# Cross-attention with feed-forward on one core: loads on one queue, setup copies on ScalarE, and a last sum begun by TensorE

## The chip, the cores and the metric

The kernel runs on 1 core of one Trainium2 chip. The metric is the device time of one execution in microseconds; of the kernel before, three runs are given. A profile of one execution of it was taken as well. Its times are counted in microseconds (us) from the start of the span.

The engines are named as in the profile: PE is TensorE (matmuls; its weight loads, PEld, are listed apart), DVE is VectorE, ACT is ScalarE, POOL is GpSimd and SP is SyncE, which issues the loads and the stores.

## The reference

The input is x of 2 x 1024 x 256, a context of 2 x 77 x 256, a mask of 1024 x 77, and the weights of one attention layer with 16 heads and of eight feed-forward experts, of which only the first has a weight in the result. Cut to what matters:

```python
def attention(x, y, mask, Wq, bq, Wk, bk, Wv, bv, Wo, bo):
    q = (x @ Wq + bq).reshape(B, T, 16, 16)
    k = (y @ Wk + bk).reshape(B, 77, 16, 16)
    v = (y @ Wv + bv).reshape(B, 77, 16, 16)
    att = 0.25 * einsum('bthd,bThd->bhtT', q, k)
    att = softmax(att * mask - 1e10 * (1 - mask))
    return einsum('bhtT,bThd->bthd', att, v).reshape(B, T, 256) @ Wo + bo

def ffn(t, w1, b1, w2, b2, gamma, beta):   # expert 0 alone
    z = t + relu(t @ w1 + b1) @ w2 + b2
    return layernorm(z) * gamma + beta

x = x + attention(layernorm(x), ctx, mask, ...)
x = x + ffn(layernorm(x), ...)
```

All of it is float32.

## The kernel before

The 2048 rows of x are cut into eight tiles of 256 rows, called halves (h = 0 to 7); a half holds two rows on each of 128 partitions (n = 0, 1). Each half goes through one chain of stages. A stage is a short function that issues one group of instructions on one engine.

The attention side of a half: `xst`, `xrs`, `xnm`, `xn` (statistics, power and norm of x), `px` (turned by TensorE, L375), `xh` and `xl` (its high part rounded by ScalarE, L380, and the rest by VectorE, L385: a product in full precision is made of three matmuls, high by high, high by low, low by high), `pq` (query projection, L397), `qh` (query bias, L405), and for each n `sc` (scores, L417), `mu` (times the mask, DVE, L429), `bi` (plus the mask's bias, POOL, L438), then the maxima of eight heads each (`mx`, L443, and `ma`, L448), the subtraction for the first eight heads on DVE (`sb`, L453) and for the other eight on ScalarE (`sa`, L459, one instruction for each head), four turns (`tr`, L468) with four exponentials (`ex`, L473). Then `po` (times the values, L481; a column of ones beside the values gives the sums), `on` (division, L493 to L498), `pot`, `oh`, `ol`, `px1` (output projection, L529).

The feed-forward side: `yst` (residual sum and statistics), `yrs`, `ynm`, `tg` (norm), `py`, `yh`, `yl`, four up projections (`up`, L571) with `re` (relu, L580), `hh` (high part, L585) and `hl` (low part, POOL, L589), four down projections (`dn`, L600), then `zst` (sum with the residual, L612, and statistics, L329 to L333), `zrs` (power, POOL, L337), `znm`, `zt`, `zs` (norm, gamma and beta) and `out` (store, L642). The last half is stored in two parts, n = 0 and n = 1; for it the norm is made by two VectorE instructions for each part, L634 and L636.

What is done once: `wq`, `wk` are loaded through ScalarE's queue (L238, L239), everything else through SP's. The context is turned (`pc`, L278) and copied (`ct`, L284, DVE); the keys are projected (`pk`, L290) and spread into blocks with their bias by four VectorE instructions (`kb`, L296); the values are projected (`pv`, L308) and their bias, which was loaded to all 77 partitions, is added (`vs`, L311, DVE). The weights of the projections and of the feed-forward are cut into a high part (`fh`, L266, ScalarE) and a low part (`fl`, L269, POOL) once they have landed.

The order of the work on every engine is worked out beforehand by a planner (class `Stages`). Each stage has an engine, a cost, the stages it comes after, the buffers that it takes (rings, PSUM banks), and a rank; whenever an engine is free in the plan, the ready stage with the lowest rank is taken. The rank of a stage of half h is START[h], plus the costs on the path to it, plus TILE_LAG for the later stages, plus an offset for its name from the table LATER. The instructions are then issued in that order, and each engine takes its own in order; waits come from the data.

Fillers (`wm`, L210) are matmuls on zeros. They have the last rank of all, are ready one after the other by GAP, and take TensorE where the plan has nothing else for it.

## Time and profile before

| | us |
|---|---|
| median of 3 runs | 210.77 (210.18 to 211.86) |
| profiled execution, whole | 211.81 |
| its span, first to last instruction | 210.0 |

Some of the groups, as count and mean duration of one:

| group | count | mean, ns |
|---|---|---|
| POOL, bias of the scores, L438 | 32 | 1399 |
| POOL, low part of the hidden tile, L589 | 32 | 1289 |
| POOL, low parts of w1 and w2, L269 | 8 | 1294 and 1293 |
| ACT, subtraction for one head, L459 | 128 | 357 |
| ACT, high parts of w1 and w2, L266 | 8 | 624 and 626 |
| DVE, key blocks, L296 | 4 | 371 |
| DVE, values plus bias, L311 | 2 | 405 |
| DVE, last norm, L634 and L636 | 2 each | 489 and 484 |

Busy times are shares of the whole span. Since matmuls overlap, the busy time of PE tells where it had work and not how well it used it. In a row of the timeline the numbers are start and length in us, then engine, line, operation, the tile written, the tiles read, and in brackets how long the engine was idle before and what ended that.

### The profile page before, as it was taken

To read this page: it belongs to the slowest core of one execution; us is meant where nothing else is said; L and a number is where in the kernel's file an instruction comes from. 1 tells how busy PE (TensorE), PEld (TensorE's weight loads), DVE (VectorE), ACT (ScalarE), POOL (GpSimd) and SP (SyncE) were. 2 spreads that over 40 slices of the span, in tenths; PEclk is the share of its full clock that TensorE was granted. 3 is DMA by queue.
4 is the path that set the end of the run, shared out by engine and by line. 5 is a ranking of instruction groups with operands and counts; after the bars stand their busy time and mean duration, and the time that the engine had idled before them with its cause. 6 is when DMAs were issued, how large, how long until landed. Compare 5 with 4: busy or idle time off the path is not lost. (4 is left out here: it accounts for less than half of the span.)

```text
span 210.0 us, 4829 instructions
## 1 busy us (share of the span) xinstructions
PE 201.2 (96%) x1852; PEld 175.9 (84%) x1852; DVE 154.8 (74%) x336; ACT 155.3 (74%) x386; POOL 149.1 (71%) x151
## 2 busy tenths in 40 slices
PE   6999769999999999999999999999999999999995
PEld 1778556987996999799999778999988979999981
DVE  1678996999767992769999768999487667267234
ACT  3289998899894699993789997259997857624910
POOL 3469999899999967869998180197976573653741
PEclk9999997999999999999999999999999999999999
DMA  5997000000000000010000100001010000101011
GB/s 194 356 396 262 0 3 3 2 0 3 0 0 3 3 2 0 3 50 3 2 0 3 50 5 0 3 0 50 3 50 3 0 0 5 50 0 52 3 50 52
DMA packets 4807, 8.73 MB, mean 42 GB/s; under 512 B 662, under 2 KB 995, under 8 KB 4784
## 3 DMA queue, kind: packets, MB, share of 16 engines
q1 hardware_dynamic: 4496, 7.90, 10.3%
q10 hardware_dynamic: 288, 0.52, 0.7%
q8 instruction: 14, 0.23, 0.5%
q14 instruction: 9, 0.07, 0.1%
HBM read 6.33 MB, written 2.10 MB: 40 GB/s over the span
## 5 line engine op out<-in xcount | busy, mean ns | idle before, releaser
L438 POOL TENSOR_TENSOR u<-u,mb 128x616 f32<-128x616 f32 x32 | 44.1, 1399 | 9.5 <-DVE u L429 9.1
L589 POOL TENSOR_TENSOR hl<-h,hh 128x512 fp32r<-128x512 f32 x32 | 40.9, 1289 | 10.2 <-ACT hh L585 8.7
L571 PE MATMUL ps<-yh,w1h 128*128 128x256 f32 x128 | 37.4, 292 | 0.0
L473 ACT ACTIVATE pT<-ps 77x512 f32<-77x512 f32 x64 | 34.2, 593 | 3.9 <-PE ps L468 3.9
L600 PE MATMUL ps<-w2h,hh 128*128 128x256 f32 x128 | 37.0, 289 | 0.0
L468 PE MATMUL ps<-ident,u 128*77 128x128 f32 x256 | 34.9, 281 | 2.1 <-DVE u L453 1.3
L571 PE MATMUL ps<-yl,w1h 128*128 128x256 f32 x128 | 36.3, 283 | 0.0
L571 PE MATMUL ps<-yh,w1l 128*128 128x256 f32 x128 | 36.1, 282 | 0.0
L600 PE MATMUL ps<-w2h,hl 128*128 128x256 f32 x128 | 35.8, 279 | 0.0
L600 PE MATMUL ps<-w2l,hh 128*128 128x256 f32 x128 | 35.8, 279 | 0.0
L468 PEld LDWEIGHTS ps<-ident,u 128*77 128x77 f32 x256 | 29.5, 150 | 6.6 <-DVE u L453 2.2
L459 ACT ACTIVATE u<-u,mx 128x77 f32<-128x77 f32 x128 | 33.7, 357 | 0.6 <-DVE mx L448 0.6
L580 ACT ACTIVATE h<-ps,cols 128x256 f32<-128x256 f32 x64 | 26.6, 471 | 7.9 <-DVE ot L493 3.8
L571 PEld LDWEIGHTS ps<-yh,w1h 128*128 128x128 f32 x128 | 24.4, 191 | 1.7 <-issue 0.9
L429 DVE TENSOR_TENSOR u<-ps,mk 128x616 f32<-128x616 f32 x32 | 24.1, 792 | 2.0 <-PE ps L417 2.0
L600 PEld LDWEIGHTS ps<-w2h,hh 128*128 128x128 f32 x128 | 24.3, 190 | 1.2 <-issue 1.1
L571 PEld LDWEIGHTS ps<-yl,w1h 128*128 128x128 f32 x128 | 24.5, 191 | 0.2 <-DVE yl L554 0.2
L571 PEld LDWEIGHTS ps<-yh,w1l 128*128 128x128 f32 x128 | 24.5, 191 | 0.0
L600 PEld LDWEIGHTS ps<-w2l,hh 128*128 128x128 f32 x128 | 24.1, 188 | 0.0
L600 PEld LDWEIGHTS ps<-w2h,hl 128*128 128x128 f32 x128 | 24.1, 188 | 0.0
L585 ACT ACTIVATE hh<-h 128x512 fp32r<-128x512 f32 x32 | 20.0, 634 | 5.1 <-PE ps L600 4.5
L481 PE MATMUL ps<-pT,vb 77*32 77x256 f32 x256 | 16.8, 388 | 0.1
(96 smaller groups left out, 427.2 us busy)
## 6 DMA issues: line engine op xcount, KB each, us to landing
x<-in_x SPq DMA_DIRECT2D x8, 256.0 KB, 5.5
out<-tg SPq DMA_DIRECT2D x7, 256.0 KB, 2.0
wst<-in_L_ffn_w SPq DMA_DIRECT2D x4, 256.0 KB, 5.4
wst<-in_w SPq DMA_DIRECT2D x4, 256.0 KB, 6.0
rows<-in_rows SPq DMA_DIRECT2D x1, 512.0 KB
mk<-in_mask SPq DMA_DIRECT2D x1, 308.0 KB, 4.9
wq<-in_wq ACTq DMA_DIRECT2D x1, 256.0 KB
wk<-in_wk ACTq DMA_DIRECT2D x1, 256.0 KB, 4.6
```

The costliest lines, as they stand in the source:

```text
L429: nc.vector.tensor_tensor(us[h, n][:, 8 * s : 8 * s + 8].rearrange("p (b h) t -> p b h t", b=2), ps[:, b0 : b0 + 2, :W].rearrange("p b (h ...
L438: nc.gpsimd.tensor_tensor(v, v, mb[:, h % HPB, n].unsqueeze(1).to_broadcast([P, 8, T]), ALU.add)
L459: nc.scalar.activation(u, u, AF.Identity, bias=mx[:, k : k + 1])
L468: nc.tensor.transpose(pt[:T, j], us[h, n][:, k], ident)
L473: nc.scalar.activation(pTs[h][:, i, :, n], pss.pop(("t", h, n, i))[:T], AF.Exp)
L481: nc.tensor.matmul(pos[h, s][r, e], lhsT=vb[:, h // HPB, k], rhs=pTs[h][:, 2 * s + e, j].rearrange("k n t -> k (n t)"), start=True, stop=True,
L571: nc.tensor.matmul(pz[:, i], lhsT=w[:, c, j * P : (j + 1) * P], rhs=v[:, c], start=(k == 0), stop=(k == 5))
L580: nc.scalar.activation(t[:, i], pz[:, i], AF.Relu, bias=b1[:, 2 * q + i : 2 * q + i + 1])
L585: nc.scalar.activation(hh[h, q], hs[h, q], AF.Copy)
L589: nc.gpsimd.tensor_tensor(hl[h, q], hs.pop((h, q)), f(hh[h, q]), ALU.subtract)
L600: nc.tensor.matmul(pys[h, ns[0]][:, n], lhsT=v[h, q][:, i, n * P : (n + 1) * P], rhs=w[:, j], start=(q == 0 and n == ns[0] and i == 0 and ...
```

## The change

Loads. `wq` and `wk` are loaded from SP too, and the order there is x0, context, wk, mask, wq, x1, wv, x2, value bias, wo and then as before. The small table of columns (biases, b1, block mask) is packed behind the mask, in one load of 640 columns, and has no load of its own. The value bias is loaded to one partition.

Setup. The context copy and the key blocks are made by ScalarE (the key blocks with a scale and a bias from columns, the bias multiplied beforehand by one small VectorE instruction, `bkm`). The value bias is added by a third matmul, a row of ones by the bias row, and the values are then copied by ScalarE.

Last half. Each of its two parts gets a sum that TensorE begins with the residual (`dt`, an identity matmul of 256 columns), so the VectorE addition goes. The centring (`zc`) is a stage of its own that does not come after the power. The low parts of its last two hidden tiles are made by VectorE instead of POOL.

Order. The subtraction on ScalarE is two stages of four heads, one for each of the turns that read it; the maximum of the first eight heads comes after the first bias stage alone; all START, LATER, TILE_LAG and several costs have other values, and the planner's delay between two engines no longer falls away where two stages merely begin with the same letter. Fillers are 256 columns wide in place of 512, there are 100 in place of 40, ready every 0.3 in place of 0.44, with a cost of 0.11 in place of 0.3.

```diff
-START = [0.0, 19.8, 51.7, 142.9, 83.1, 131.4, 163.5, 235.6]
+START = [0.0, 73.7, 67.8, 216.8, 128.7, 156.8, 213.7, 271.1]
...
-WARM = 40
+WARM = 100
...
-GAP = 0.44
-TILE_LAG = 11.6
+GAP = 0.3
+TILE_LAG = 19.8
...
-        return 0.0 if k[0] == u[0] else HOP[self.all[k]["eng"] + self.all[u]["eng"]]
+        return 0.0 if self.name(k) == self.name(u) else HOP[self.all[k]["eng"] + self.all[u]["eng"]]
...
+    LAST = [(NH - 1, q) for q in (2, 3)]
...
+        nc.tensor.matmul(bank(("wm", i))[:, :256], lhsT=zero[:, :P], rhs=zero, start=True, stop=True)
...
+    mkc = const([P, a["mask"].shape[1]], "mkc")
+    mk = mkc[:, : HPB * 2 * T].rearrange("p (h n t) -> p h n t", h=HPB, n=2)
+    cols = mkc[:, HPB * 2 * T :]
...
-    load_matrix("wq", "wq", "hh", nc.scalar)
-    load_matrix("wk", "wk", "hl", nc.scalar)
...
-        nc.vector.tensor_copy(ct, pcv)
+        nc.scalar.activation(ct, pcv, AF.Copy)
...
+    def k_bias():
+        nc.vector.tensor_tensor(
+            bkm, bk.unsqueeze(2).to_broadcast([P, 2, 2]), bm.unsqueeze(1).to_broadcast([P, 2, 2]), ALU.mult
+        )
+
+    def k_blocks(c):
+
+        for e in range(2):
+            nc.scalar.activation(
+                kb[:, :, c, e], pss["k"][:, c], AF.Identity, bias=bkm[:, c, e : e + 1], scale=bm[:, e : e + 1]
+            )
...
+        nc.tensor.matmul(pv, lhsT=one, rhs=bv, start=False, stop=True)
+
+    def v_copy(b):
+        nc.scalar.activation(vb[:, b, :, :D], pss.pop(("v", b)).rearrange("p (h d) -> p h d", d=D), AF.Copy)
...
+    def s_sub_act(h, n, i):
+        for k in heads(i):
             u = us[h, n][:, k]
-            nc.scalar.activation(u, u, AF.Identity, bias=mx[:, k : k + 1])
+            nc.scalar.activation(u, u, AF.Identity, bias=mxs[h, n, 1][:, k : k + 1])
...
+        eng = nc.vector if (h, q) in LAST else nc.gpsimd
+        eng.tensor_tensor(hl[h, q], hs.pop((h, q)), f(hh[h, q]), ALU.subtract)
...
-        nc.vector.tensor_tensor(y2, y2, tg[h][:, n0:n1], ALU.add)
+        if h < NH - 1:
+            nc.vector.tensor_tensor(y2, y2, tg[h][:, n0:n1], ALU.add)
         stats(y2, f"z{h}_{n0}")
+
+    def z_center(h, n):
+        y2 = pys[h, n][:, n]
+        nc.vector.scalar_tensor_tensor(y2, y2, sts[f"z{h}_{n}"][0][:, 0, 0:1], gamma, ALU.subtract, ALU.mult)
+
+    def f_first(h, n):
+
+        pys[h, n] = bank(("dt", h, n), (P, 2, E))
+        nc.tensor.matmul(pys[h, n][:, n], lhsT=ident, rhs=tg[h][:, n], start=True, stop=False, skip_group_check=True)
...
-            half("mx", "V", 0.1 + 0.08 * (H - ACT_HEADS[h]), [("bi", n, 0), ("bi", n, 1)], s_max, n, lag=lag)
...
+            half("mx", "V", 0.74, [("bi", n, 0)], s_max, n, lag=lag)
...
+                if i >= 2:
+                    half("sa", "S", 1.0, [("ma", n)], s_sub_act, n, i, lag=lag)
```

Of the table LATER, the offsets that the text speaks of: `fl` (low parts of w1 and w2) from 64.8 to 127.9, `up` from 25.5 to 80.7.

## The prediction

> **What bounds the kernel now.** I read the page first, then the busy times by stretch, the timeline of the opening and of the end, and the waits of TensorE. The page says that TensorE is the engine to follow, and the stretches say where it is not full.
>
> ```profile
> PE 201.2 (96%) x1852; PEld 175.9 (84%) x1852; DVE 154.8 (74%) x336; ACT 155.3 (74%) x386; POOL 149.1 (71%) x151
> ```
> ```profile
> 0.00:12.20 12.20, 10.00 (x36) 5.83 (x37) 5.87 (x20) 4.71 (x9) 4.32 (x14) 1.00 0.82 291
> 12.20:30.00 17.80, 14.52 (x142) 11.51 (x141) 16.01 (x34) 17.02 (x45) 16.84 (x23) 1.00 0.42 157
> 30.00:110.00 80.00, 79.56 (x785) 71.26 (x784) 65.06 (x136) 66.86 (x173) 71.97 (x68) 0.98 0.01 5
> 110.00:203.40 93.40, 92.99 (x877) 85.72 (x877) 64.38 (x139) 66.70 (x163) 54.82 (x47) 1.00 0.05 18
> 203.40:210.00 6.60, 4.08 (x19) 1.56 (x16) 3.50 (x11) 0.00 (x0) 1.10 (x2) 1.00 0.12 41
> ```
>
> Columns: length, then PE, PEld, DVE, ACT, POOL busy. From 30 to 203.4 us TensorE is busy for 172.55 of 173.4 us: work added to it there lengthens the kernel, and work taken from others there gives nothing. What can be won lies in three places: before the first query projection (12.25 us), between 12.2 and 30, and after 203.4.
>
> The front, from the timeline (start, length, engine, line):
>
> ```profile
> 4.54 0.75 DVE L329 BATCH_NORM_STATS2 st_x<-x 128x6 f32<-128x256 f32 x2 [3.39 <-DMA x<-in_x]
> 5.91 2.34 PE L210 MATMUL ps<-zero 128*128 128x512 bf16 x5
> 6.34 0.47 DVE L284 COPY ct<-ps 128x308 f32<-128x308 f32 x1
> 7.22 1.09 ACT L357 ACTIVATE xn<-x,nm_x,rs_x 128x256 f32<-128x256 f32 x2 [1.85 <-DVE nm_x L342]
> 8.04 2.18 PE L290 MATMUL ps<-ct,wk 128*128 128x154 f32 x8
> 10.05 0.60 PE L375 MATMUL ps<-ident,xn 128*128 128x128 f32 x4
> 12.25 0.47 PE L397 MATMUL ps<-xh,wqh 128*128 128x256 f32 x1
> ```
>
> The first tile of x lands at 4.54. Its normed rows are ready at 8.31, but their turn on TensorE starts at 10.05, behind the key projection (8.04). That one had its input at 6.81 and stood behind five filler matmuls: TensorE takes its queue in order.
>
> The opening and the end:
>
> ```profile
> 21.95 1.03 PE L210 MATMUL ps<-zero 128*128 128x512 bf16 x4
> 24.25 1.10 PE L468 MATMUL ps<-ident,u 128*77 128x128 f32 x8 [1.27 <-DVE u L453]
> 28.91 0.80 PE L417 MATMUL ps<-kb,qs 32*128 32x154 f32 x12 [1.80 <-ACT pT L473]
> ```
> ```profile
> 202.75 0.43 DVE L612 TENSOR_TENSOR ps<-ps,tg 128x256 f32<-128x256 f32 x1 [3.87 <-PE ps L600]
> 203.14 0.28 PE L600 MATMUL ps<-w2h,hl 128*128 128x256 f32 x1
> 203.99 0.42 DVE L612 TENSOR_TENSOR ps<-ps,tg 128x256 f32<-128x256 f32 x1
> 205.44 0.55 POOL L337 TENSOR_TENSOR rs_z<-rs_z,mhalf 128x1 f32<-128x1 f32 x1 [0.74 <-DVE rs_z L333]
> 206.79 0.48 DVE L636 SCALAR_TENSOR_TENSOR tg<-ps,rs_z,x 128x256 f32<-128x256 f32 x1
> ```
>
> Idle or filled with nothing in the opening: 1.03 + 1.27 + 1.80 = 4.1 us. At the end, 3.85 us pass from the last matmul's end (203.42) to the last scale's end (207.27), then 2.7 us of store and closing.
>
> **The change, part by part**, against the profiled run (211.81 us, 210.0 of it span; the median of the three runs is 210.77, 1.04 below).
>
> *Loads.* x0 shared the wires with wq, issued by ScalarE at the same moment. Around 4 to 6 us the DMA table shows some 400 GB/s, so 256 KB less ahead of it is 0.64 us: x0 lands at 3.9. c (154 KB) follows 0.4 later, 4.3, where before it ended TensorE's wait at 5.37. wq now comes behind c, wk and mask with columns (about 730 KB, 1.8 us after 4.54): 6.4 us; its two copies (0.63 and 0.69) end near 8, and it is needed at 10. x1 moves behind mask and wq, 0.3 MB or 0.8 us later; its rows waited 1.2 us for ScalarE (0.30 and 1.66 of statistics end near 10.4, xn starts at 11.70), which hides it. The ACT issues (0.41 and 0.39) vanish, two issues of 0.38 to 0.43 go to SP ahead of all later loads, and the column load (0.35) goes. Total bytes stay, so the last weights land as before.
>
> *Front.* From 3.9, statistics and norm take the same 3.77: 7.7. The context turn (0.75) from 4.3, its copy and the key projection (2.18) end near 8.0. Then turn, high part, low part take the 2.20 of before (10.05 to 12.25): query projection at 10.2, 2.05 earlier. One filler in the way costs some 0.2; I take **-1.8**, bounds 0 (fillers as badly placed as the five above) and -2.05.
>
> *Copies on ScalarE.* The context copy (0.47 on DVE) falls into ScalarE's idle time (4.71 of 12.2 busy). The key blocks were four DVE instructions of 0.371 and become four on ScalarE of 154 elements with two column operands: between the 128x77 row with one (0.357) and the 128x256 row with two (0.603), 1.4 to 2.4 in all; near 8 to 10.5 ScalarE waited 2.38 us for the turn, so they cost nothing unless the high part (0.60) stands behind a pair of them, then up to 1.2. The value copies (two, about 0.45 by the 128x256 rows) fall into the opening, where ScalarE is busy for 17.02 of 17.80.
>
> The Trainium skill ("ScalarE: Activation LUTs", Rules for kernel authors) speaks against this part: it sends plain adds and multiplies to VectorE. By its figures (about 0.19 us fixed, 0.09 for each column operand, 0.83 ns an element) one key block is, as an estimate, 0.50 us, so 2.0 for four against 1.5 before; in this trace it is the load of the two engines in that stretch that decides.
>
> *Value bias by matmul.* Two more matmuls of 256 columns: two of this kind took 1.03 (L308), so 0.5 each. One lies in the front's idle time (behind it are fillers), the other in the dense opening: **+0.5**, bounds 0 and +1.0.
>
> *Opening.* The maximum of the first eight heads no longer stands behind the second bias add (1.40 on POOL), the ScalarE subtraction is cut into two fours, so a turn may follow the first four (1.05 earlier), and the weights' low parts (1.29 each on POOL; one, at 14.81, stands ahead of the first bias add at 17.73) sink in rank. Against it: ScalarE and POOL (16.84 of 17.80) are both nearly full. Bounds: -4.1 and, with the value copies on the path, +0.9. I take half of what is idle, **-2.0**.
>
> *Middle.* The order is redrawn; TensorE's instructions stay. 0 with the bounds -2 (TensorE hardly idles, only its mixing of kinds can tighten) and +6 (rival below).
>
> *Last half.* Two identity matmuls of 256 columns on a TensorE that is full: **+0.9** (0.43 to 0.52 each by the same L308 row), bounds 0 and +1.0. They replace the DVE add (0.43 and 0.42). The last low parts on DVE (0.69 for 1.29) fall into its 3.87 us of waiting; without that cover they would put 0.69 ahead of the statistics. After the last matmul remain: a hop of 0.25 (as from 12.00, the end of xl, to 12.25), statistics 0.43, and from there as 203.22 to 204.70 shows for the first part (aggregate, epsilon, power), then 0.1 and the scale of 0.48; the centring (0.49) fits beside the power (0.55). That is 2.35 for 3.85; DVE still holds the first part's centring, up to 0.5. **-1.2**, bounds -1.5 and -0.8.
>
> *Fillers.* 100 for 40, half as wide. Before, 18 were left for the end and finished at 208.23, short of the store. At 0.108 each, 60 left over would run 6.5 us after the last matmul, against some 5.3 for the rest: 0, up to +1.5.
>
> Sum: -1.8 + 0.5 - 2.0 + 0.9 - 1.2 = -3.6; 208.2 for the profiled run, **207.2** for the median.
>
> The clock: seven fillers take 3.17 us from 1.21 (0.43 apart), five take 1.24 from 10.49 (0.22 apart), while the granted clock reads 1.00 throughout. So TensorE speeds up between 7.6 and 10.5. The Trainium skill ("TensorE: Matmul & The Clock Gate", Part 1) has a rule that speaks against the change: half rate until about 3.4 us of sustained activity, and again after as long an idle time; thinner fillers, planned every 0.30 us where they ran 0.43 long every 0.44, are less sustained. If the fast rate came only after the first query projection, that one (12 matmuls 0.12 apart, 1.44) would take twice as long by these two spacings, and the sum would be -2.2.
>
> **The rivals.**
>
> A, the forecast, 207.2 (205.7 to 209.2): 0.46, of it 0.40 faster and 0.06 same.
>
> B, more: the opening gives all 4.1 and the middle 1.5: -7.2, **203.6**. For it: maxima, subtractions and turns may all start earlier. Against it: 172.55 of 173.4. 0.17, all faster.
>
> C, the opening stays, since ScalarE and POOL are its bound: -1.6, **209.2**. For it: 17.02 of 17.80. 0.12; 0.03 faster, 0.09 same.
>
> D, slower: POOL becomes the bound, because the low parts of the feed-forward weights come too late. There are eight at 1.29 (10.3 us). For it: POOL is the fullest helper from 30 to 110 (71.97 of 80), and the lateness of these copies goes from 64.8 to 127.9, while that of the up projection that reads them goes from 25.5 to 80.7. Against it: the four of w1 ended at 43.0 and the first up projection began at 52.0, the four of w2 ended at 52.9 and the first down projection began at 67.3, so 9 and 14 us can be lost first. Each copy that TensorE stands and waits for is +1.29: three (3.9) eat the whole gain, and from there D decides; five, w1's four and one of w2's, are +6.45, **213.7**; all eight 217.5. 0.20, all slower.
>
> E, the change does at the front what it says, but the fillers left over end the kernel: +1.5, **208.7**. For it: 60 more of them. 0.05, same.
>
> **How the numbers follow.** 207.2 is A's. Range 203.4 to 213.0: below it lies what is left of B if the middle gives its whole 2 (0.07), above it D from five whole copies on (0.13 of its 0.20; the other 0.07 is the fifth half hidden, +5.8, 213.0). Over 1% faster (under 208.66): 0.40 + 0.17 + 0.03 = 0.60; within 1%, about what a measurement of this kernel can tell from no change: 0.06 + 0.09 + 0.05 = 0.20; slower 0.20.
>
> **What would show it.** x0 landing near 3.9 and the first L397 row near 10.2; TensorE busy for over 16 of the 17.8 us that follow; TensorE as dense from 30 us to the last matmul as before; 2.4 to 2.9 us from the last matmul to the last scale; low-part copies done before the first up projection, with no wait of TensorE for POOL. Wrong: a first query projection after 11.5, waits of TensorE for POOL or ScalarE of several us between 30 and 200, or fillers that end after the last store.

## The result, and the profile after

| | before | after |
|---|---|---|
| median, us | 211.31 (20 runs, 210.18 to 212.95) | 212.45 (20 runs, 211.26 to 214.72) |
| profiled execution, whole | 211.81 | 212.64 |
| its span | 210.0 | 210.8 |

The ratio is 1.0059, with a 95% interval of 1.0038 to 1.0080: the change made the kernel slower by 0.6%. The forecast was 207.2, faster with a chance of 0.60. Medians are of all runs, ratios leave out the runs in which the chip was in a slower state, and e9 and e16, which were profiled in that state, are read by their times alone.

The page's line of busy times for the kernel after:

```profile
PE 202.5 (96%) x1920; PEld 180.3 (86%) x1920; DVE 151.7 (72%) x331; ACT 159.2 (76%) x393; POOL 146.5 (69%) x149
```

TensorE is as busy as before, 202.5 against 201.2, in 68 more matmuls. Sixty of them are fillers, so the sum hides what is useful. The stretches of the kernel after (length, then PE, PEld, DVE, ACT, POOL busy with their counts, granted clock, DMA):

```profile
0.00:12.12 12.12, 10.16 (x55) 6.59 (x56) 5.22 (x21) 7.36 (x15) 4.79 (x15) 1.00 0.84 293
12.12:30.00 17.88, 15.77 (x156) 13.99 (x156) 13.77 (x29) 15.16 (x37) 16.69 (x22) 1.00 0.44 152
...
30.00:60.00 30.00, 29.39 (x327) 23.59 (x325) 29.11 (x55) 29.16 (x82) 29.46 (x29) 1.00 0.01 2
...
110.00:200.10 90.10, 90.10 (x837) 84.57 (x835) 59.07 (x133) 62.80 (x150) 50.44 (x44) 1.00 0.04 16
200.10:202.60 2.50, 2.50 (x25) 2.24 (x24) 1.94 (x7) 1.07 (x2) 1.24 (x2) 1.00 0.00 0
...
206.07:210.80 4.73, 1.11 (x11) 0.75 (x8) 1.67 (x5) 0.00 (x0) 0.55 (x1) 0.89 0.08 29
```

Two rows matter. From 200.1 to 202.6 TensorE is "full", but with fillers, as the timeline of the end shows (start, length, engine, line):

```profile
199.98 0.28 PE L600 MATMUL ps<-w2h,hl 128*128 128x256 f32 x1
200.11 2.69 PE L212 MATMUL ps<-zero 128*128 128x256 bf16 x23
201.81 0.48 DVE L643 SCALAR_TENSOR_TENSOR tg<-ps,rs_z,x 128x256 f32<-128x256 f32 x1 [0.19 <-POOL rs_z L339]
202.63 0.60 PE L623 MATMUL ps<-tg,ident 128*128 128x256 f32 x2
...
205.79 0.28 PE L600 MATMUL ps<-w2h,hl 128*128 128x256 f32 x1
205.91 1.27 PE L212 MATMUL ps<-zero 128*128 128x256 bf16 x10
206.11 0.43 DVE L331 BATCH_NORM_STATS2 st_z<-ps 128x6 f32<-128x256 f32 x1 [2.29 <-PE ps L600]
207.69 0.48 DVE L643 SCALAR_TENSOR_TENSOR tg<-ps,rs_z,x 128x256 f32<-128x256 f32 x1 [0.33 <-POOL rs_z L339]
```

Between the last part's first sum (done at 200.1) and the identity matmul that begins its second sum (202.63) stand 23 fillers, in the queue of an engine that takes its work in order. And in the row from 30 to 60 all four engines are busy for over 29 of 30 us, where before DVE had 25.75 and ACT 27.68.

The front, from the timeline of the kernel after:

```profile
3.47 0.75 DVE L331 BATCH_NORM_STATS2 st_x<-x 128x6 f32<-128x256 f32 x2 [2.38 <-DMA x<-in_x]
3.99 0.75 PE L283 MATMUL ps<-ident,c_sb 77*128 77x77 f32 x4 [0.18 <-DMA c_sb<-in_c]
5.26 1.32 PE L295 MATMUL ps<-ct,wk 128*128 128x154 f32 x8
5.83 1.09 ACT L359 ACTIVATE xn<-x,nm_x,rs_x 128x256 f32<-128x256 f32 x2 [0.62 <-DVE nm_x L344]
7.18 0.60 PE L377 MATMUL ps<-ident,xn 128*128 128x128 f32 x4
...
7.54 0.63 ACT L271 ACTIVATE wqh<-wq 128x512 fp32r<-128x512 f32 x1 [0.61 <-DMA wq<-in_wq]
8.07 1.58 ACT L307 ACTIVATE kb<-ps,bkm,mkc 128x154 f32<-128x154 f32 x4
...
9.53 0.61 ACT L382 ACTIVATE xh<-ps 128x512 fp32r<-128x512 f32 x1
10.52 1.09 PE L314 MATMUL ps<-wv,ct 128*77 128x256 f32 x4
10.55 0.66 DVE L387 TENSOR_TENSOR xl<-ps,xh 128x512 fp32r<-128x512 f32 x1
...
12.12 0.38 PE L399 MATMUL ps<-xh,wqh 128*128 128x256 f32 x1
```

x lands at 3.47 (4.54 before) and is turned by 7.78 (10.65 before, by the rows of 10.05 and 0.60), yet the first query projection begins at 12.12 (12.25). The turned rows wait 1.75 us for ScalarE, which waits for wq until 7.54 and then makes the four key blocks; and TensorE has the value projections in front.

In what follows, **TensorE's lag** at a time t is t less the time that the computation's own matmuls done by then take at the pitch at which they follow each other densely; fillers count nothing. It is worked out from the matmul records, and less lag at the same t is more work done.

| t, us | lag before | lag after |
|---|---|---|
| 34 | 20.73 | 18.81 |
| 40 | 21.00 | 20.85 |
| 60 | 22.79 | 22.94 |
| 200 | 28.71 | 27.93 |

So TensorE was 1.9 us ahead at 34 us, lost that by 40, won 0.9 between 60 and 200, lost 2.5 in the fillers at 200, paid 0.86 for two identity matmuls, and won 1.74 behind the last matmul (206.07 to 208.18, where it was 3.85): +0.8, the spans' difference. Part of the 1.9 isn't the change's: in the execution before, the granted clock of TensorE was 0.81 from 28 to 32 us and 0.76 from 32 to 36, in the one after 1.00.

### The profile page after: what moved, and what is told of

It reads as the page before. It is cut to its first block, busy times and chain, and to the rows that moved or that the text cites. A ratio compares the mean times of both kernels' runs of the same rounds, so it can differ in the third digit from the quotient of the medians.

```text
span 210.8 us, 4973 instructions
## 1 busy us (share of the span) xinstructions
PE 202.5 (96%) x1920; PEld 180.3 (86%) x1920; DVE 151.7 (72%) x331; ACT 159.2 (76%) x393; POOL 146.5 (69%) x149
## 4 chain that ended last, share of the span: by engine, by line
PE 82%; DMA 8%; DVE 3%; ACT 3%; issue 1%; SPq 1%; POOL 0%; POOLq 0%
PE ps L600 22%; PE ps L570 22%; PE ps L467 12%; PE ps L480 8%; PE ps L528 6%; PE ps L419 5%; DMA x<-in_x 4%; PE ps L399 3%; DMA mkc<-in_mask 2%; DMA wst<-in_L_ffn_w 2%; PE ps L212 2%; PE ps L544 2%; ACT pT L472 1%; DVE u L431 1%; ACT u L458 1%
## 5 line engine op out<-in xcount | busy, mean ns | idle before, releaser
L589 POOL TENSOR_TENSOR hl<-h,hh 128x512 fp32r<-128x512 f32 x30 | 38.7, 1294 | 11.9 <-ACT hh L584 10.8
L472 ACT ACTIVATE pT<-ps 77x512 f32<-77x512 f32 x64 | 35.1, 591 | 10.5 <-PE ps L467 10.5
L600 PE MATMUL ps<-w2h,hh 128*128 128x256 f32 x128 | 37.7, 295 | 0.0
L458 ACT ACTIVATE u<-u,mx 128x77 f32<-128x77 f32 x128 | 34.7, 359 | 1.1 <-DVE mx L449 0.9
L579 ACT ACTIVATE h<-ps,mkc 128x256 f32<-128x256 f32 x64 | 26.6, 470 | 8.8 <-PE ps L570 7.7
L467 PEld LDWEIGHTS ps<-ident,u 128*77 128x77 f32 x256 | 29.0, 147 | 4.9 <-issue 2.5
L431 DVE TENSOR_TENSOR u<-ps,mkc 128x616 f32<-128x616 f32 x32 | 24.2, 791 | 7.8 <-PE ps L419 7.8
L339 POOL TENSOR_TENSOR rs_z<-rs_z,mhalf 128x2 f32<-128x2 f32 (+1 forms) x9 | 6.0, 666 | 27.9 <-DVE rs_z L335 27.5
L570 PEld LDWEIGHTS ps<-yh,w1h 128*128 128x128 f32 x128 | 24.5, 191 | 1.0 <-issue 1.0
L570 PEld LDWEIGHTS ps<-yl,w1h 128*128 128x128 f32 x128 | 24.5, 191 | 0.0
L570 PEld LDWEIGHTS ps<-yh,w1l 128*128 128x128 f32 x128 | 24.5, 191 | 0.0
```

The lines of the kernel that those rows point to most:

```text
L431: nc.vector.tensor_tensor(us[h, n][:, 8 * s : 8 * s + 8].rearrange("p (b h) t -> p b h t", b=2), ps[:, b0 : b0 + 2, :W].rearrange("p b (h ...
L458: nc.scalar.activation(u, u, AF.Identity, bias=mxs[h, n, 1][:, k : k + 1])
L467: nc.tensor.transpose(pt[:T, j], us[h, n][:, k], ident)
L472: nc.scalar.activation(pTs[h][:, i, :, n], pss.pop(("t", h, n, i))[:T], AF.Exp)
L570: nc.tensor.matmul(pz[:, i], lhsT=w[:, c, j * P : (j + 1) * P], rhs=v[:, c], start=(k == 0), stop=(k == 5))
L579: nc.scalar.activation(t[:, i], pz[:, i], AF.Relu, bias=b1[:, 2 * q + i : 2 * q + i + 1])
```

## The experiments

All ratios are to the kernel before, with 95% intervals. All but e7 are edits of the kernel after. `move(stages, behind)` puts stages behind another one in the finished order of issue; nothing else of the order changes. Times of stages are of the profiled executions.

### The fillers at the end: e1

```diff
-        for key in st.order():
+        order = st.order()
+        order = [key for key in order if key[0] != "wm" or key[1] < 67]
+        for key in order:
```

> The changed kernel in its own order, without the 33 fillers from the 67th on (23 of them stand on TensorE between the first part's down projections and the identity matmul of the second part, 200.1 to 202.6 us). Theory (the fillers are the cost): the plan left a hole there, because the second part's sum may only begin when one of two sums is given back, and filled it; on the chip the data of the second part are there, so TensorE goes straight on: the identity matmul near 200.2, the end 2.3 to 2.5 us earlier, about 1.1 to 1.2% less than the changed kernel. Rival (the hole is real): the second part waits for a low part, a bank or a scale until about 202.5; then TensorE stands idle instead, and the time moves by less than 0.3 us.

Measured: 210.62, ratio 0.9963 [0.9933, 0.9993]. The timeline of e1 at the same place:

```profile
199.75 0.28 PE L600 MATMUL ps<-w2h,hl 128*128 128x256 f32 x1
199.87 0.59 PE L623 MATMUL ps<-tg,ident 128*128 128x256 f32 x2
...
205.07 0.48 DVE L643 SCALAR_TENSOR_TENSOR tg<-ps,rs_z,x 128x256 f32<-128x256 f32 x1 [0.33 <-POOL rs_z L339]
```

The identity matmul follows at once: nothing on the chip had held it, neither data nor bank. What held it was the plan, which allows two sums open at a time:

```python
SUMS = 2
half("dt", "P", 0.45, ["yb"], f_first, *ns, lag=lag, banks=[[("zs",) + ns]], sums=("dn", SUMS))
```

Half 3's sum and the last half's first part held both places, so the second part's `dt` had to come, in the plan, after the scale of the first. TensorE was free in the plan meanwhile, and the planner issued fillers there. They are real instructions; on the chip 2.5 us of them ran where useful work was ready. This is shown: the last scale came 2.6 us earlier (205.55 for 208.18). The step stands in one place: TensorE's own matmuls have the same order in both kernels, the same matmul starts 0.24 us earlier in e1 from 24 us on to 198, and 2.76 earlier from the identity matmul on.

### The other fillers, the copies, the queue of wq and wk: e10, e11, e12, e14

```diff
# e10, in place of the 67 of e1
+        order = [key for key in order if key[0] != "wm" or key[1] < 27]
# e11, on e1; the copies of the values likewise
-        nc.scalar.activation(ct, pcv, AF.Copy)
+        nc.vector.tensor_copy(ct, pcv)
...
-            nc.scalar.activation(
-                kb[:, :, c, e], pss["k"][:, c], AF.Identity, bias=bkm[:, c, e : e + 1], scale=bm[:, e : e + 1]
+            nc.vector.tensor_scalar(
+                kb[:, :, c, e], pss["k"][:, c], bm[:, e : e + 1], bkm[:, c, e : e + 1], ALU.mult, ALU.add
# e12, on e1; these two are no longer loaded from SP
+    load_matrix("wq", "wq", "hh", nc.scalar)
+    load_matrix("wk", "wk", "hl", nc.scalar)
```

e14 is e10, e11 and e12 together.

> The kernel of e1 without the 40 fillers between the first query projection and 50 us as well (7 at 14 to 15.4, 16 at 25 to 28.7, 16 at 36.7 to 38.6, 1 at 49.5). If fillers in those places also delay work that is ready, as they do at the end: up to 1 us earlier than e1 (ratio 0.991 to 0.994). If TensorE really has to wait there: within 0.3 us of e1.

> The kernel of e1 with the context copy, the key blocks and the value copies on VectorE again (same order, same loads). In the changed kernel the key blocks (1.58 us on ScalarE, 8.07 to 9.65) stood ahead of the high part of x0 that was ready at 7.8. If that is what held the front: the first query projection is only as early as the value projections ahead of it let it (11 to 11.5 instead of 12.1), and the end comes 0.5 to 1 us earlier. If the place of the copies is without weight: within 0.4 us of e1.

> The kernel of e1 with the loads of wq and wk issued by ScalarE again, ahead of everything, as in the kernel before. x0 then shares the wires with wq and lands near 4.5 instead of 3.5, the context 1 us later; wq lands near 4.7 instead of 7.5, so the high and low parts of wq and of x0 no longer stand behind it. If the earlier x0 is worth something: the first query projection and the end come later by up to 1 us. If the wait for wq cancels it: within 0.4 us of e1.

> The changed kernel without the fillers behind the 27th, with the turned mask column's copy, the key blocks' and the values' copies on VectorE, and with the query and key weights' loads issued by ScalarE's queue. If the small gains seen of each alone add: 0.9963 without late fillers, 0.0009 for the other fillers, 0.0014 for the copies and 0.0033 for the second queue, a ratio of 0.9907 or about 209.4 us. If they are the same gain seen three times (each only makes the front start earlier or TensorE's queue shorter, and the opening takes it back): 0.993 to 0.995, 209.8 to 210.3 us.

Measured: e10 210.43, 0.9954 [0.9923, 0.9985]; e11 210.15, 0.9949 [0.9927, 0.9972]; e12 209.81, 0.9930 [0.9901, 0.9959]; e14 209.98, 0.9945 [0.9923, 0.9968]. All overlap with e1's interval and with each other. Neither the engine of the early copies nor the queue of wq and wk has an effect that these runs tell from none, and together they give no more than one of them. What all of them share is the removal of the late fillers, and all of them beat both kernels, by 0.4 to 0.7% under the kernel before. The fillers at 25 to 28.7 and at 36.7 to 38.6, which e10 leaves out as well, held nothing: the same matmul of TensorE starts 1.18 us earlier in e10 than in the kernel after at 24 us, ahead of them, and 1.25 earlier at 40, behind them.

### The front alone: e2 and e8

```diff
# e2
+        move([("kb", 0), ("kb", 1)], ("xh", 0))
+        move([("pv", 0), ("vs", 0), ("pv", 1), ("vs", 1)], ("pq", 0))
+        move([("xst", 2), ("xrs", 2)], ("xl", 0))
# e8, 14 more fillers ahead of the first query projection
+        for i in range(14):
+            order.insert(order.index(("pq", 0)), ("more", i))
```

> The changed kernel in its own order, except at the front: the key blocks come after the high part of the first tile on ScalarE, the value projections after the first query projection on TensorE, the third tile's statistics after the first low part on VectorE. Theory (order at the front ate the gain of the earlier load): the first query projection starts at 9.6 to 10.2 instead of 12.12, and if TensorE is the bound from there on, the end comes 1.9 to 2.5 us earlier. Rival (the opening is bound by the other engines): the first query projection starts as early, but the progress of TensorE at 40 us and the end move by less than 0.7 us.

> The changed kernel in its own order, with 14 more fillers of 0.108 us on TensorE ahead of the first query projection, so that it starts 1.5 us later. If TensorE's front sets the time, as the prediction's front term took it: 1.5 us slower, 0.7%. Rival (the opening has a chain of its own, and the front has slack): at 22 us TensorE is as far as without them, and the end moves by less than 0.4 us.

e2: 214.24, 1.0121 [1.0071, 1.0172]; e8: 213.89, 1.0120 [1.0080, 1.0160]. ScalarE's timeline in e2:

```profile
8.21 0.60 ACT L382 ACTIVATE xh<-ps 128x512 fp32r<-128x512 f32 x1 [0.50 <-PE ps L377]
8.71 1.59 ACT L307 ACTIVATE kb<-ps,bkm,mkc 128x154 f32<-128x154 f32 x4
...
13.69 0.38 ACT L318 ACTIVATE vb<-ps 77x256 f32<-77x256 f32 x1 [1.12 <-PE ps L315]
15.29 0.38 ACT L318 ACTIVATE vb<-ps 77x256 f32<-77x256 f32 x1 [1.22 <-PE ps L315]
15.57 1.08 ACT L359 ACTIVATE xn<-x,nm_x,rs_x 128x256 f32<-128x256 f32 x2
16.55 0.82 ACT L407 ACTIVATE qs<-ps,mkc 128x256 f32<-128x256 f32 x2
```

The first query matmul came at 8.87 as meant and the rest by 12.2, but its bias on ScalarE (L407) came at 16.55, behind two copies of values that TensorE now made late. The wait moved one stage on. The Trainium skill ("TensorE: Matmul & The Clock Gate", Part 1, Architectural detail) says that ScalarE and VectorE take their queues strictly in order; these rows agree: the bias had its input by 12.3 and ran 4.2 us later. e8 holds the front back by 1.3 to 1.5 us and is 0.6% (1.3 us) slower than the kernel after by the two ratios, whose intervals just touch. Its trace is level with the kernel after at 22 us (lag 14.47 for 14.38) and 0.44 behind at 34 (19.25 for 18.81); the table of the next section shows that these 0.44 go with a later load and not with the fillers. So whether the front held back costs time, or has slack, stays open.

### What is late in the opening, one stage at a time: e3, e4, e5, e6

```diff
# e3
+        move([("fh", k) for k in range(4, 8)], ("yl", 0))
# e4
+        move([("xb", 2), ("xb", 0), ("xb", 1)], ("bi", 2, 1, 1))
# e5
+        for h in (3, 4, 5, 6):
+            move([("xb", h)], order[order.index(("px1", h)) - 25])
# e6
+        move([("xst", 4)], ("mu", 0, 1, 1))
```

`xb` is the addition of the output projection's bias to x, on POOL.

> The changed kernel in its own order, except that the four high parts of w2 (0.62 us each on ScalarE, at 20.4 to 23.0) come after the first low part of the feed-forward input, near 48 us. If ScalarE bounds the opening: turns and exponentials come up to 2.5 us earlier and the end 1 to 2.5 us. If POOL bounds it, or the chain through mask, bias and maximum: less than 0.4 us, perhaps worse by as much, since ScalarE has them to do later.

> The changed kernel in its own order, except that three output-bias adds on POOL (1.28 us each; two of them at 16.1 to 18.7 stand ahead of the first score bias, which began at 18.64 while its input was there at 17.3; one at 21.3) come after the eighth bias pair, near 39 us. If POOL bounds the opening: the first score bias starts at 17.3, the first turn 1.3 to 2.6 us earlier, the end 1 to 2.5 us earlier. If ScalarE bounds it: less than 0.4 us.

> The changed kernel in its own order, except that the output-bias adds of halves 3 to 6 (1.28 us each on POOL, at 31.3, 39.2, 40.5 and 47.9 us) come shortly before the output projection that needs them, after 60 us. Theory (all helpers are full in the opening, POOL the most: it works without a pause from 16.1 to 60): with 5.1 us less on POOL before 60, TensorE gets its turns earlier and is 1 to 4 us further at 60 us, and the end comes 1 to 3 us earlier. Rival (the opening goes by ScalarE, or by all three alike): less than 0.5 us at 60 us, and the adds moved into the middle cost what they gain.

> The changed kernel in its own order, except that the statistics of half 4 on VectorE, which stood idle 1.93 us for the load of that half (landed at 19.9), come after the two mask products that stood behind them (21.5 to 23.0). Theory (a load in the way of the masks holds the opening, as the chain of waits says): masks start at 20.0, scores at 20.8 instead of 22.3, and the end comes 0.8 to 1.5 us earlier. Rival (POOL is full anyway): the masks come earlier, but the second pair of bias adds starts at 22.6 as before, and the end moves by less than 0.4 us.

Measured: e3 214.33, 1.0153 [1.0101, 1.0205]; e4 214.82, 1.0127 [1.0070, 1.0185]; e5 213.3, 1.0107 [1.0073, 1.0141]; e6 213.68, 1.0110 [1.0068, 1.0153]. None is faster than the kernel after. In e4, e5 and e6 the lag at 60 us was 24.93, 23.61 and 24.93 instead of 22.94. In e3 it was 17.47 instead of 18.81 at 34 us and 21.13 instead of 22.40 at 52.

e3's lead looks like the gain of four copies less on ScalarE, and it isn't. The rows of the kernel after (first fence) and of e3 (second) show what the first turn waited for:

```profile
19.90 0.75 DVE L331 BATCH_NORM_STATS2 st_x<-x 128x6 f32<-128x256 f32 x2 [1.93 <-DMA x<-in_x]
...
23.72 1.10 PE L467 MATMUL ps<-ident,u 128*77 128x128 f32 x8 [0.61 <-DVE u L453]
24.42 1.08 ACT L472 ACTIVATE pT<-ps 77x512 f32<-77x512 f32 x2 [1.38 <-PE ps L467]
```
```profile
18.58 0.75 DVE L331 BATCH_NORM_STATS2 st_x<-x 128x6 f32<-128x256 f32 x2 [1.16 <-DMA x<-in_x]
...
22.40 1.10 PE L467 MATMUL ps<-ident,u 128*77 128x128 f32 x8 [0.61 <-DVE u L453]
23.10 1.08 ACT L472 ACTIVATE pT<-ps 77x512 f32<-77x512 f32 x2 [2.48 <-PE ps L467]
```

The statistics of half 4 stand on VectorE ahead of the second pair of masks and of the first subtraction, and wait for their load. In e3's execution it landed 1.32 us earlier, the first turn came 1.32 earlier, and ScalarE, with four copies less, only waited longer for it (2.48 for 1.38). e10, which has the four copies in their old place, has the same lead. The table takes the kernels in which TensorE's own matmuls have the order of the kernel after, and gives how much later (+) or earlier (−) than there the same matmul starts:

| | statistics of half 4 | of that wait for the load | first turn | at 24 us | at 40 | at 60 | at 198 |
|---|---|---|---|---|---|---|---|
| after | 19.90 | 1.93 | 23.72 | 0 | 0 | 0 | 0 |
| e1 | 19.09 | none | 23.48 | −0.23 | −0.26 | −0.24 | −0.24 |
| e3 | 18.58 | 1.16 | 22.40 | −1.32 | −1.32 | −0.61 | −0.24 |
| e4 | 21.07 | 2.07 | 24.88 | +1.16 | +1.13 | +1.85 | +2.48 |
| e5 | 19.77 | none | 24.20 | +0.48 | +0.48 | +0.50 | +0.50 |
| e8 | 20.33 | 1.13 | 24.15 | +0.43 | +0.44 | +0.45 | +1.20 |
| e10 | 18.70 | 0.86 | 22.54 | −1.18 | −1.25 | −1.25 | −1.25 |

Where VectorE waits for the load, the distance at 24 us is the difference in its landing to within 0.02 us (after, e3, e4, e8, e10), though none of these edits moves a load. And what stands at 24 us is carried to the end in e1, e5 and e10; e4 and e8 lose more on the way, and e3 loses its lead. So e5 shows more than its lag says: 5.1 us less on POOL before 60 us moved TensorE by nothing between 24 and 198 us. e6 takes the wait out of the way of the masks, but the statistics then stand (22.62) ahead of the first subtraction, which comes at 23.50 instead of 22.88.

e3 keeps its lead until ScalarE makes the four copies, at 54.7 to 56.9, and loses 1.07 of 1.31 us between 58 and 65 us, where e10 loses nothing. Two stretches of e3:

```profile
28.00:52.00 24.00, 23.39 (x253) 19.28 (x251) 23.32 (x45) 23.57 (x66) 23.23 (x27) 1.00 0.01 2
52.00:62.00 10.00, 9.87 (x107) 6.44 (x104) 8.77 (x16) 10.00 (x27) 8.77 (x8) 1.00 0.01 2
```

Where the four copies run, ScalarE (the fourth busy time) has no idle time at all, and VectorE and POOL have 1.2 each: more work on ScalarE there holds TensorE up. That the median is 0.9% over the kernel after's is not explained by the trace, whose span (210.9) is level with it; the profiled execution was the fastest of e3's six (212.66).

### The first softmax ahead: e9, e13, e15, e16, e17

Each of these orders moves several stages of half 0's chain forward and others back, e9 on e1, the others on e14. Of each the moves that matter; e17 has all of e15:

```diff
# e9
+        move([("kb", 0), ("kb", 1)], ("xh", 0))
+        move([("xst", 1), ("xrs", 1), ("xst", 2), ("xrs", 2)], ("xl", 0))
+        move([("pv", 0), ("pv", 1), ("vs", 0), ("vs", 1)], ("ex", 0, 0, 1))
...
# e13
+        move([("sc", 0, 0)], ("xn", 2))
+        move([("pv", 1)], ("xl", 2))
+        move([("pv", 0)], ("xl", 3))
...
# e15
+        move([("kb", 0), ("kb", 1), ("xst", 2), ("xrs", 2)], ("xl", 0))
+        move([("sc", 0, 0), ("pv", 0), ("pv", 1), ("mu", 0, 0, 0), ("mu", 0, 0, 1)], ("xh", 1))
+        move([("xl", 1), ("vs", 0), ("xst", 3), ("vs", 1), ("bi", 0, 0, 0), ("bi", 0, 0, 1)], ("mu", 0, 0, 1))
+        move(["wol", ("xrs", 3)], ("bi", 0, 0, 1))
...
# e16, on e15: fillers up to the 16th in place of the 27th
+        order = [key for key in order if key[0] != "wm" or key[1] < 16]
# e17, on e15
+        move([("sb", 0, 0), ("ma", 0, 0)], ("mx", 0, 0))
+        move([("tr", 0, 0, 0), ("tr", 0, 0, 1)], ("pq", 1))
...
```

> The kernel of e1 (the change without its late fillers) with the whole opening put in order of the first half: key blocks behind the high part of x0, the statistics of halves 1 and 2 behind its low part, the value projections and their copies moved from ahead of the first query projection into the fillers' place near 25 us (17 fillers there go), two output-bias adds behind the first two score biases on POOL, the statistics of half 4 behind the first subtraction. Theory (the prediction's front and opening terms, 1.8 and 2.0, were there, and the order on the queues lost them): first query projection near 10, first score bias on POOL near 14.5 instead of 18.6, first turn near 20 instead of 23.7, and the end 2 to 4 us before that of e1 (ratio to the kernel before 0.978 to 0.987). Rival (all three helpers are full until 60 us, so only the sum of their work counts): the first turn comes as early, but TensorE's progress at 60 us and the end move by less than 0.8 us (ratio 0.992 to 0.999).

> The next kernel (e14: no fillers behind the 27th, the three copies back on VectorE, the query and key weights' loads issued by ScalarE) with the order of half 0's whole chain made first: on VectorE the key blocks behind the low part of half 0's input, the statistics of half 2 behind those; on TensorE both value projections behind the second and third turns of the input, and the first scores ahead of the turn of half 2; on POOL the first two output-bias adds behind half 0's score biases; the statistics of half 4 behind half 0's subtraction. Theory that the queues' order is what kept the predicted gain of the front and the opening away: the first query projection by 11, the first score bias by 15 instead of 18.6, and at 60 us TensorE 1.5 to 3 us further than in e14; the time 1.5 to 3 us under e14's, a ratio near 0.98 to the kernel before. Rival, that the helpers' sum of work up to 60 us sets the pace and order only shifts it: the first softmax up to 3 us earlier but TensorE level with e14 at 60 us, and the time within 0.6 us of e14's.

> The kernel of e14 with half 0's chain ahead on every queue, and now without the slip of e13, where the first masks stood on VectorE behind the low parts of halves 1 and 2 (scores done at 15.5, first mask at 19.7). VectorE: low part of half 0, key blocks, statistics of half 2, both masks of the first scores, then low part of half 1 and the rest. TensorE: first query projection, turn of half 1, first scores, then the two value projections, in the time in which it would wait for half 2. POOL: the first two score biases ahead of the output weights' low part, the statistics of half 3 and the first two output-bias adds. Theory (order alone): first score bias by 16 (18.9 in e14), first turn of probabilities by 21.5 (23.6 in e14), and TensorE at 60 us 1.5 to 2.5 us ahead of e14; time 1.5 to 2.5 us below e14's 209.98. Rival (the helpers' sum of work sets the pace): first turn ahead by as much, level with e14 at 60 us, time within 0.6 us of e14's.

> e15 without the fillers that stand on TensorE between the key projection and the first query projection (7 before the turn of half 0's input, 4 behind it; in e14 the turn's input was ready at 7.8 and the turn ran at 9.7, behind seven of them). If they delay ready work: the first query projection up to 1.5 us earlier than in e15, and with the theory that order decides, up to 1.5 us of time; with the rival nothing. If they keep TensorE at its rate: the query projection takes up to twice as long (3.4 us for 1.7) and the front is no earlier.

> e15 with the rest of the first softmax ahead as well: in e15 the first score bias came at 15.7, as expected, but the first subtraction stood on VectorE behind masks that waited for the second scores (23.8 instead of 19.2), and the first turn came at 24.6. Here the subtraction and the first maximum for ScalarE stand directly behind the first maximum, the first two turns behind the second half's query projection, the exponentials and ScalarE's own subtractions behind the query biases, and the third output-bias add behind half 0's last score bias. Theory (order alone): first turn by 20.5, TensorE at 60 us 1 us or more ahead of e14, time at least 1 us under e14's 209.98. Rival (the helpers' work up to 60 us sets the pace): first turn by 20.5 as well, but TensorE at 60 us level with e14 or behind it (a lag of 22.9 or more), time 209.5 or more.

Measured: e9 213.28, 1.0060 [1.0020, 1.0101]; e13 222.26, 1.0525 [1.0495, 1.0554]; e15 212.5, 1.0080 [1.0049, 1.0110]; e16 210.98, 1.0004 [0.9976, 1.0031]; e17 214.65, 1.0167 [1.0117, 1.0217]. e9, whose trace isn't read, tells only that its moves gain nothing. From the traces of the others, with e14 beside them, busy times from 12 to 60 us:

| | first turn | ScalarE | VectorE | POOL | lag at 60 | ratio |
|---|---|---|---|---|---|---|
| e14 | 23.6 | 44.35 | 44.20 | 46.51 | 22.94 | 0.9945 |
| e15 | 24.6 | 42.99 | 43.76 | 43.74 | 24.69 | 1.0080 |
| e17 | 20.6 | 39.80 | 40.61 | 40.66 | 28.44 | 1.0167 |
| e13 | 31.0 | 33.81 | 34.25 | 34.59 | 33.65 | 1.0525 |

e13 and e15 each left a stage out of place (masks behind two low parts; the first subtraction behind masks that waited for later scores), so they tell little of the first softmax. e17 has its first turn 3.0 us earlier than e14, as expected, and is 2.2% slower. Its first stretches:

```profile
12.00:30.00 18.00, 15.06 (x123) 11.15 (x123) 12.69 (x30) 12.85 (x32) 11.60 (x15) 1.00 0.40 147
30.00:60.00 30.00, 27.05 (x256) 22.23 (x260) 27.91 (x54) 26.95 (x73) 29.06 (x33) 0.89 0.01 2
```

The helpers did less by 60 us than in e14 and TensorE is as far behind as they are: an early first softmax is worth nothing if the engines behind it then wait. The column that goes with the lag is ScalarE's: 1.36, 4.55 and 10.54 us less of it than in e14 go with 1.75, 5.50 and 10.71 us more lag. VectorE's and POOL's columns fall in the same kernels, so this table doesn't tell the three apart. Nor does it tell them from TensorE's own rate: from 12 to 60 us the granted clock was 0.93 in e17 and 0.82 in e13, and 1.00 in e14 and e15, so in the two slowest part of the lag is a slower TensorE. e16, which is e15 without eleven of the front's fillers, is 1.5 us faster than e15, and their intervals are apart, so those eleven cost time too; whether by delaying ready work, no trace here shows. Whether e14 gains by the same removal wasn't tried.

### POOL made lighter: e18

```diff
+        order = [key for key in order if key[0] != "xb"]
```

> e14 without the additions of the output projection's bias to the input (this leaves that bias out of the result): eight POOL instructions of 1.25 us, seven of them before 60 us, so 8.8 us less of POOL's 46.5 busy in the 48 us from 12 to 60 (ScalarE 44.4, VectorE 44.2 there); the order of everything else stays. The first query projection and the first scores stay where e14 has them. Theory now (POOL's load, with VectorE's and ScalarE's close behind it, sets the pace to 60 us): TensorE at 60 us 1.5 to 3.5 us ahead of e14 (a lag of 19.4 to 21.4 instead of 22.9) and a time 1.5 to 3.5 us under e14's 209.98. Rival (the chain to the first softmax, or TensorE's own work, sets it): the two adds ahead of the first score bias, 2.5 us, come off the first turn, but the lag at 60 us within 0.5 us of e14's and the time within 0.6 us.

Measured: 210.21, 0.9948 [0.9921, 0.9975], level with e14. From 12 to 60 POOL was busy for 38.22 instead of 46.51, and the lag is the same as e14's at 30, 34, 40 and 60 us (22.94). Stretches of e18:

```profile
12.00:30.00 18.00, 16.00 (x136) 13.57 (x136) 15.35 (x32) 15.04 (x36) 14.38 (x23) 0.91 0.41 148
30.00:60.00 30.00, 28.49 (x308) 22.13 (x308) 28.22 (x53) 29.16 (x83) 23.84 (x22) 1.00 0.01 2
```

From 30 to 60 POOL idles for 6.2 of the 30 us, VectorE for 1.8, and nothing comes earlier: POOL doesn't set the pace there, as in e5, and the theory under which e18 was made falls. (Before 28 us the two executions differ for a reason of their own, told in the last section.) ScalarE stays at 29.16. In the kernel after, these two lines of the table of waits are all that ScalarE waited for another's result from 30 to 60:

```profile
ACT xh L382 <- ACT qs L407: 0.4, 1, 0.4
ACT h L579 <- PE ps L570: 0.4, 1, 0.4
```

### The last half alone: e7

The edit of the last half on the kernel before: the sum begun by an identity matmul, the centring beside the power, the last low parts on VectorE.

```diff
+            if h == NH - 1:
+                nc.tensor.matmul(
+                    pys[h, ns[0]][:, ns[0]], lhsT=ident, rhs=tg[h][:, ns[0]], start=True, stop=False, skip_group_check=True
+                )
...
-        nc.vector.tensor_tensor(y2, y2, tg[h][:, n0:n1], ALU.add)
+        if h < NH - 1:
+            nc.vector.tensor_tensor(y2, y2, tg[h][:, n0:n1], ALU.add)
```

> The kernel before with its own order, loads and setup, and of the change the last half alone: the identity matmul that begins each part's sum (issued with the part's first down projection), no addition on VectorE, the centring right after the statistics, two low parts on VectorE. By the terms measured in the changed kernel: +0.86 for the two matmuls on TensorE and -1.75 from the last matmul to the last scale, so -0.9 us, 0.4% faster than before. If the two matmuls hide behind waits of the last half: -1.5. If the gain at the end belongs to the new order: 0 to +0.9.

Measured: 211.46, 1.0011 [0.9979, 1.0044]. The last scale ends 2.55 us behind the last matmul instead of 3.85, and the last matmul ends at 203.99 instead of 203.42: a gain of 0.7 in this profile (last scale at 206.54 for 207.28), of which the times show nothing: +0.2 us, with an interval of 0.7 to either side. The 0.9 us that the expectation took from the changed kernel lies outside it, so the gain at the end doesn't show as time in the order of before.

## Why the prediction was wrong

The likeliest case said 207.2, and the range (203.4 to 213.0) held the time by luck, on the side on which only rival D was. D was not the cause: in the kernel after the low parts of w1 ended at 55.6 and the first up projection began at 57.2, those of w2 ended at 65.9 and the first down projection began at 71.4, and TensorE waited for POOL nowhere between 30 and 200 us. By the terms of the sum:

- **Fillers, 0 predicted, +2.5 measured. This step failed, and it alone turns the sign.** The prediction asked what fillers left over would do *behind* the last matmul; ten ran there (205.91 to 207.2) and cost nothing, since the last scale ends at 208.18. It didn't ask where the plan would have nothing else for TensorE though the chip would. That was ahead of the second part's sum, which the plan's two open sums made wait. e1 shows the cause and the size, 2.52 us at this one place.
- **Front, −1.8 predicted, −0.13 measured.** x landed even earlier than predicted (3.47 for 3.9) and its rows were turned at 7.78. The step that failed is "the key blocks cost nothing unless the high part stands behind a pair of them, then up to 1.2" together with wq at 6.4: ScalarE waited for wq until 7.54, and the high part stood behind all four blocks (8.07 to 9.65). Then the first query projection stood behind the value projections, of which the prediction had counted only the bias matmuls. e2 took these out of the way, and the next stage on ScalarE was late instead. The −0.13 is one execution: among the kernels whose front is that of the kernel after to the instruction, the first query projection began at 11.56 (e3), 13.36 (e1) and 14.07 (e5), never near 10.2. In e1 the high part stood behind nothing (9.98, the turn ended at 9.94); there TensorE's rate, which doubled 4 us later (last section), was most of what made the front late.
- **Opening, −2.0 predicted, 0 measured at 60 us.** The step that failed is a term put at nothing: the prediction has maxima, subtractions and turns start earlier, and no wait for a load ahead of them. In the new order half 4's statistics stand ahead of them on VectorE and waited 1.93 us for their rows. Where the rows came 1.2 us earlier, in e10, the first turn came 1.18 earlier and TensorE kept 1.25 us to 198 us, so a gain at this place counts in full. What the kernel after had won over the kernel before by 34 us was not kept: from 36.7 to 38.9 it ran 15 fillers, because what it waited for was not made. Rival C ("the opening stays, since ScalarE and POOL are its bound") was right in its outcome. From 30 to 60 us ScalarE had 0.8 us of idle time; e5 and e18 exclude POOL as the bound, and e3 shows TensorE falling back when ScalarE has more to do. A run that takes work off ScalarE from 30 to 60 us for good wasn't made, so ScalarE as the only bound is likely and not shown; VectorE, at 29.11 of 30, is close behind.
- **Value bias by matmul, +0.5.** Both bias matmuls turned out to lie in front of the first query projection, so their cost is inside the front's −0.13; it was not measured by itself.
- **Middle, 0 predicted, −0.9 measured** from 60 to 200 us, inside its bounds.
- **Last half, +0.9 and −1.2 predicted; +0.86 and −1.74 measured.** In the profile mechanism and cost were right, and the gain was larger than its bound of −1.5: the statistics began 0.04 behind the end of the last matmul, not a hop of 0.25. (The prediction's own parts add up to 2.31 us behind the last matmul, where it wrote 2.35; 2.11 were measured.) That the last half by itself saves time is not shown: e7's time is level with the kernel before.

Without the 2.5 us of fillers the terms as measured give −0.78 (the lags at 200 us) + 0.86 − 1.74 = −1.7 us of span. e1's profiled span is 208.2 for 210.0; its ratio says less, −0.8 us (−0.1 to −1.4). So even then the change would have been worth under half of the 3.6 that the sum gave. The rule of the Trainium skill ("ScalarE: Activation LUTs", Rules for kernel authors) on plain arithmetic, weighed in the prediction, decides nothing here: e11, which follows it, has 0.9949 beside e1's 0.9963.

## What to carry to other kernels

A filler is an instruction in an in-order queue: it may stand only where the chip, and not just the plan, has nothing to run, so look in the trace at what is issued directly behind each run of fillers and whether its inputs were there. A first stage that starts earlier is worth what the next in-order queue behind it lets through; before pricing it, list what stands ahead of each later stage on its engine. Where the engines run without idle time behind a first stage, the time of that stage is carried to the end (1.25 us from 24 to 198 us in e10), so look for the wait that ends last ahead of it, here a load in the queue of VectorE. And a single profile tells which wait ended last in that execution; it doesn't rank kernels: of twelve runs of e10 the profiled one was the second fastest (208.97, median 210.43), of twelve of e12 the slowest (211.12, median 209.81).

## What the runs showed of the hardware that was not expected

TensorE doubles its rate at a time that differs between executions of the same instructions. In e14 the key projection (eight matmuls at 6.46) took 2.35 us, in e18, whose front is the same code, 1.32 (at 6.42), and the first query projection began at 13.7 and 12.35. The granted clock reads 1.00 for the whole front of both kernels before and after, so the rate has to be read from the spacing of matmuls. Rows of e18's timeline show the slow rate again later, 24.5 us in, after 0.91 us of idle time, with 0.21 from one to the next where e14 has 0.12 (here the granted clock shows it too, 0.57 from 24 to 28 us):

```profile
24.49 0.55 PE L401 MATMUL ps<-xh,wqh 128*128 128x256 f32 x1 [0.91 <-DVE xl L389]
24.84 0.42 PE L401 MATMUL ps<-xl,wqh 128*128 128x256 f32 x1
25.05 0.41 PE L401 MATMUL ps<-xh,wql 128*128 128x256 f32 x1
```

That took back the 1.1 us by which e18's first turn was ahead (22.5 for 23.6): the turns behind this projection begin at 27.18 in e18 and at 27.1 in e14. The Trainium skill ("TensorE: Matmul & The Clock Gate", Part 1) explains a step that moves by a window of activity that runs free of the kernel, and puts the spread at half a microsecond to either side, for sustained activity. Here the fillers went from 0.21 apart to 0.11 at 5.0 us in the kernel after and at 9.2 in e1, whose instructions are the same up to 200 us, so the measured difference is about 4 us; in both fronts TensorE also stood idle for a load (0.18 and 0.66 us ahead of the turn of the context).
